# Joins of 64-row blocks laid out by value head, and the loads of layer 1's FFN weights moved into layer 1's order

## The chip, the cores and the metric

The kernel runs on one core of one Trainium2 chip. It is one Bass/Tile program. The metric is device microseconds (us) of one execution, as the median over several runs. A change of about 0.2% of this kernel's time (3.5 us) is about what its measurement can tell from no change.

## What is computed

The input x holds 2 batches of 512 tokens with 256 features (f32). Four layers follow one another, each of the form `x = x + attention(layernorm(x)) + ffn(layernorm(x))`:

- layer 0: attention with 16 query and 4 key heads, and a mixture of 8 experts of which each token takes 2
- layer 1: ALiBi attention, and a gated FFN with Hadamard transforms (weights up, gate and down, together W1F, 3 MB)
- layer 2: linear attention, and a second mixture of experts (weights W2)
- layer 3: a gated delta rule with 16 key heads and 32 value heads, and an FFN whose weights come from a look-up table

The delta rule works in chunks of 64 tokens in the reference. Cut to what matters here:

```python
L = -matmul(k_beta, k.T) * decay            # strictly lower triangular, one per head and chunk
attn = solve_triangular(eye - L, eye, lower=True)
v_intra = matmul(attn, v_beta)
k_cumdecay = matmul(attn, k_beta * exp(g_cum))
# then a scan over the chunks carries a state from chunk to chunk
```

The inverse `attn` of a unit lower triangular matrix is what the changed code computes.

## The kernel before

**The order of the work.** Every part of the kernel is a generator that issues a few instructions and yields. For layers 0 to 2 the order in which the generators advance is written out by hand in strings (ORDER0, ORDER1, ORDER2, L63 on): `weave_in` (L342) takes the next step of the stream that each letter names. In layer 3 every stream has a list of places (JOIN, L1607, is the one of the joins), and `weave_at` (L334) goes through all of them in the order of place. The scheduler is told to keep the order. Each engine, and each queue of DMA requests on SyncE (SP) or GpSimd (POOL), then works strictly in the order in which its instructions were issued. All ordinary matmuls go through the helper `mm` (L116), so they are told apart by the names of their operands.

**Layer 3.** The kernel uses chunks of 128 tokens. A unit is one key head and one batch: 2 value heads x 4 chunks = 8 matrices (NM) of 128x128 to invert. There are 32 units. For the first 24, roughly, the work of several units stands side by side: PE projects and convolves (pxv, pxq, pz), VectorE (DVE) runs the 31-step solve of the 32x32 diagonal blocks (tmp, xx, L1340 to L1343), and the scan of an older unit runs on PE, DVE and ScalarE (ACT).

`join(n)` (L1360 to L1412) puts the inverse of a 128x128 matrix together out of the inverses of its four 32x32 diagonal blocks, for all 8 matrices of a unit, in ten steps:

- ten DMAs on SP fetch the 32x32 inverses and the blocks of the matrix between them: dc, ml (2), U (4), dw (2), m6 (1)
- the 32-joins: twice 16 matmuls of 32x32 into one PSUM bank, p5, with a copy between them (q5); they alternate between row groups 0 and 64 of the array. ACT writes the results into U (L1397)
- a DVE transpose of 32x256 (L1399) puts the off-diagonal blocks of the upper 64x64 inverse into dw
- the 64-joins: 8 matmuls `p6 <- m6, dw`, all of whose operands lie in partitions 0 to 63; an ACT copy of 64x512 to q6 (L1406), which lies in partitions 64 to 127; 8 matmuls `p6 <- q6, U`, all of whose operands lie in partitions 64 to 127; an ACT multiplication by -1 of 64x512 into U (L1411)

m6 and q6 are the two halves of one tile. dw has 64 partitions and room for 8 matrices. An f32 matmul shows as two records in the profile, so a batch of 8 shows as x16.

**The boundary of layers 0 and 1.** In layer 0 each of 23 blocks of gathered rows goes through an expert (L583); its result is written to DRAM as ys (L626, on SP). When the last one has landed, `gathered` (L391) fetches each token's two rows by indirect DMAs on POOL (back, L396) and DVE adds them to x (L401). Then layer 1 begins with its normalisation. Between the two layers' code stands the load of all of layer 1's FFN weights, as one DMA of 3 MB (w1f_sb, L660), and that of W2 (L667), both on SP. `route` (L249) finds each token's experts, places and shares (`found`, L328).

## The time and the profile before

| what | us |
|---|---|
| median of the runs (lowest to highest) | 1743.78 (1742.91 to 1745.04) |
| the profiled execution, its own time | 1752.05 |
| its span, first to last instruction | 1750.3 |
| PE busy between 657 us and the end (layer 3, 1093 us) | 1046.25 |
| DVE busy in the same stretch | 893.01 |
| ACT busy in the same stretch | 740.44 |
| PE busy between 263 and 306 us (the boundary, 43 us) | 30.96 |

Times in views count from the span's start. Layer 0 lies at about 0 to 285 us, layer 1 at 293 to 526, layer 2 at 526 to 657, layer 3 behind that. PE is the matmul unit, PEld its loading of weights, PEclk the clock that was granted to it as a share of full speed; over the whole execution it was 0.977. A group such as `p<-dw,m 64*64 64x64 f32 x16` gives output and operands, the array's rows and columns, the moving operand's shape and the count of records. A chain is the work that ended last, followed back from the end, step by step, to what released it.

### The profile page before, as it was taken

How to read it: one execution, taken by the hardware profiler on the slowest of the kernel's cores; microseconds unless marked ns; L12 is line 12 of the kernel's file. 1: busy time of each engine (PE TensorE's matmuls, PEld its weight loads, DVE VectorE, ACT ScalarE, POOL GpSimd, SP SyncE). 2: the span in 40 equal slices, each digit the busy share in tenths (PEclk: the TensorE clock that was granted, in tenths of full speed). 3: DMA queues.
4: the chain of work that ended last, by engine and by line, in shares of the span. 5: the costliest groups of instructions: out<-in, count | busy, mean ns of one | idle time of the engine just before them, and what ended most of it. 6: DMA issues, size and time to landing. Idle time of an engine off the chain costs nothing.

```text
span 1750.3 us, 31855 instructions
## 1 busy us (share of the span) xinstructions
PE 1671.0 (95%) x11576; PEld 1193.0 (68%) x11576; DVE 1382.7 (79%) x3021; ACT 1003.1 (57%) x2638; POOL 246.0 (14%) x208
## 2 busy tenths in 40 slices
PE   7999997999999997979999999999999999999996
PEld 4377873656665664546777777777777777777775
DVE  6886556977767884778989889899899898886662
ACT  4644232854621113435777777777777778667674
POOL 3400004000000001101111121212121212011111
PEclk8999998999999997989999999999999999999998
DMA  5366743000002002756464555545645545334310
GB/s 199 139 241 240 257 169 142 14 1 1 1 1 94 1 1 69 217 159 181 136 184 135 162 156 152 174 136 146 191 131 162 155 151 158 87 87 111 88 49 24
DMA packets 258204, 214.53 MB, mean 123 GB/s; under 512 B 160769, under 2 KB 222721, under 8 KB 254721
## 3 DMA queue, kind: packets, MB, share of 16 engines
q1 hardware_dynamic: 256512, 208.31, 39.2%
q0 software_dynamic: 1536, 4.20, 0.7%
q8 instruction: 92, 1.51, 0.3%
q14 instruction: 64, 0.52, 0.1%
HBM read 152.69 MB, written 59.77 MB: 121 GB/s over the span
## 4 chain that ended last, share of the span: by engine, by line
PE 75%; DVE 18%; issue 3%; DMA 2%; ACT 2%; SPq 0%; POOL 0%; POOLq 0%; DVEq 0%; ACTq 0%
PE po L116 9%; PE pv L116 8%; PE pc L116 7%; PE pw L116 5%; PE pxv L116 5%; PE pz L116 5%; PE p L116 5%; PE ph L116 4%; PE pl L116 3%; PE pd L116 3%; DVE tmp L1340 3%; PE pxq L116 3%; PE pg L116 2%; PE pu L116 2%; PE pp L116 2%
## 5 line engine op out<-in xcount | busy, mean ns | idle before, releaser
L1259 DVE SCALAR_TENSOR_TENSOR cvv<-pxv,cols,cvv 128x511 f32<-128x511 f32 (+2 forms) x192 | 142.7, 746 | 5.2 <-ACT cvv L1256 0.3
L116 PE MATMUL po<-wo,yT 128*128 128x256 f32 x512 | 127.9, 394 | 2.3 <-ACT yT L1585 2.3
L197 POOL TENSOR_TENSOR rr<-ss,c_sb 128x8 f32<-128x8 f32 x32 | 58.1, 1815 | 497.2 <-DVE ss L1570 497.2
L116 PE MATMUL pxv<-xnT,wg 128*128 128x512 f32 x256 | 122.9, 604 | 0.0
L116 PE MATMUL pz<-wz,xnT 128*128 128x256 f32 x512 | 121.1, 379 | 0.0
L1340 DVE TENSOR_TENSOR tmp<-mb,xx 128x31 f32<-128x31 f32 (+15 forms) x248 | 106.8, 431 | 1.5
L1343 DVE TENSOR_TENSOR xx<-xx,tmp 128x31 f32<-128x31 f32 (+15 forms) x248 | 101.0, 407 | 8.5
L116 PEld LDWEIGHTS po<-wo,yT 128*128 128x128 f32 x512 | 94.4, 194 | 15.0 <-ACT yT L1585 3.2
L372 DVE SCALAR_TENSOR_TENSOR lw<-is,rows,lw 128x536 f32<-128x536 bf16 (+1 forms) x150 | 99.8, 665 | 5.3
L550 ACT ACTIVATE ex<-pl 128x512 f32<-128x512 f32 x128 | 66.6, 602 | 58.0 <-PE pl L116 58.0
L116 PEld LDWEIGHTS pz<-wz,xnT 128*128 128x128 f32 x512 | 92.3, 190 | 9.9
L1445 POOL TENSOR_TENSOR qg<-qk,qg 128x1024 f32<-128x1024 f32 x32 | 75.7, 2364 | 152.7 <-issue 41.8
L116 PE MATMUL pc<-w,aT 128*128 128x128 f32 x512 | 94.7, 277 | 0.0
L1286 ACT ACTIVATE e<-e,lnb 128x128 f32<-128x128 f32 x256 | 80.6, 390 | 15.6 <-POOL e L1280 15.3
L1516 DVE SCALAR_TENSOR_TENSOR r<-pw,negeg,tv 128x128 f32<-128x128 f32 x192 | 58.2, 345 | 36.4 <-PE pw L116 35.2
L1567 ACT ACTIVATE sq<-xf 128x128 f32<-128x128 f32 x256 | 80.1, 313 | 6.7 <-DVE xf L1552 0.7
L1577 ACT ACTIVATE xf<-xf,rr 128x128 f32<-128x128 f32 x256 | 81.4, 391 | 3.9 <-POOL rr L197 3.8
L116 PEld LDWEIGHTS pc<-w,aT 128*128 128x128 f32 x512 | 78.5, 194 | 2.1 <-DVE aT L1447 0.4
L1526 ACT ACTIVATE rb<-pw,bd 128x128 f32<-128x128 f32 x192 | 60.1, 365 | 26.8 <-PE pw L116 24.3
L1259 DVE SCALAR_TENSOR_TENSOR cvk<-pxk,cols,cvk 128x511 f32<-128x511 f32 (+2 forms) x96 | 71.5, 745 | 4.4 <-ACT cvk L1256 2.3
L116 PE MATMUL pc<-st,qg 128*128 128x128 f32 x384 | 74.6, 276 | 0.0
L1259 DVE SCALAR_TENSOR_TENSOR cvq<-pxq,cols,cvq 128x511 f32<-128x511 f32 (+2 forms) x96 | 71.7, 747 | 2.2
(327 smaller groups left out, 4047.9 us busy)
## 6 DMA issues: line engine op xcount, KB each, us to landing
e<-in_E SPq DMA_DIRECT2D x23, 1536.0 KB, 6.6
e<-g_rows SPq DMA_DIRECT2D x32, 512.0 KB, 4.6
m_dram<-mT SPq DMA_DIRECT2D x32, 512.0 KB, 3.5
e_dram<-e SPq DMA_DIRECT2D x32, 512.0 KB, 4.8
e1l<-e_dram SPq DMA_DIRECT2D x32, 512.0 KB, 3.6
qg<-g_rows SPq DMA_DIRECT2D x32, 512.0 KB, 3.7
k_dram<-k SPq DMA_DIRECT2D x32, 256.0 KB, 2.0
qk<-k_dram SPq DMA_DIRECT2D x32, 256.0 KB, 2.6
```

Source lines behind the costliest of these rows:

```text
L116: nc.tensor.matmul(o, lhsT, rhs, start=first, stop=last)
L372: nc.vector.scalar_tensor_tensor(lw[:, at], is_j, lut_j, lw[:, at], ALU.mult, ALU.add)
L550: nc.scalar.activation(exs[k // 2][:, k % 2], pls[k], AF.Exp, scale=HD**-0.5)
L1259: nc.vector.scalar_tensor_tensor(cv[:, back:], px[:, : S - back], conv[:, h, j, 3 - back : 4 - back], cv[:, back:], ALU.mult, ALU.add,)
L1286: nc.scalar.activation(e1f[:, m], e1f[:, m], AF.Exp, bias=lnb[:, h, b, m // C, m % C : m % C + 1])
L1340: nc.vector.tensor_tensor(t, bcast(mb[:q, j, j + 1 :], [q, r, k], 2), bcast(X[:q, j, :k], [q, r, k], 1), op=ALU.mult)
L1343: nc.vector.tensor_tensor(X[:q, j + 1 :, :k], X[:q, j + 1 :, :k], t, op=ALU.subtract)
L1445: nc.gpsimd.tensor_tensor(qg, bcast(qk[:, 0], [P, 2, S], 1), qg, op=ALU.mult)
L1516: nc.vector.scalar_tensor_tensor(r[i], pw[:, 0, i], negeg[:, h, b, i, c : c + 1], tv[i][:, c, :], ALU.mult, ALU.add)
L1526: nc.scalar.mul(wb[:, i], pw[:, 1, i], bd[:, h, b, i, c : c + 1])
L1567: nc.scalar.activation(sq, xfs[c // 2][:, c % 2, i], AF.Square, accum_out=ss[:, c, i : i + 1])
L1577: nc.scalar.mul(xf[:, j, i], xf[:, j, i], rr[:, c + j, i : i + 1])
```

## The change

**The joins.** The 64-joins are laid out by value head. The first head's four chunks have their operands in partitions 0 to 63 and the second head's in 64 to 127. Both batches of matmuls alternate between the two: top rows write the low half of p6, low rows the top half. dw and m6 become tiles of 128 partitions for four chunks, and q6 a tile of its own; a new tile, ub, holds a second copy of the lower 64x64 inverse of the second head, since that head's second join has its operands in partitions 0 to 63. The number of matmuls is the same. The transpose is done in two halves, the copy to q6 becomes 128x256, the last multiplication becomes two of 64x256, a multiplication of 32x128 into ub is added, and the DMAs of a unit go from 10 to 15. The places of JOIN stay as they were.

**The loads.** W1F is requested in two DMAs, the down part (1 MB) first and then up and gate (2 MB), by a stream of its own in layer 1's order, W2 by another one. By the issued instructions, the 1 MB goes out ahead of the last ys write and the 2 MB behind it; before, all 3 MB went ahead of the last.

**The orders.** The strings ORDER0 and ORDER1 are replaced, and `found` is filled in earlier for share and place, later for "of".

```diff
 ORDER0 = (
-    "#####$######u$''*$*$$'$$*$$(''$(*)'$,()*(,%))'(**,,)%%(%%(%))0%%000111..%1%22%-2..2&t--55&55--,&/666"
+    "#####$$######$$'u'$'*$$*$'$($*')*(($/'*)'),(,%(),*%()*,%%)()0%%%%%0001%11.12u..222.55-55t-6&&+666,&-"
...
 ORDER1 = (
-    "(((%%(**&%-*)--)--.+.-.-+%O-/-.+%...-//.'000./)/.'/%/%///)///022/0002&0%0000030223321224&&&442233&33"
+    "**'*+,*'/#+(/-/#'/,,/''00//0-/-1'Q10'//01000002'$+(22111+1)1111114241422(((222222255524444446(6655(("
...
         w1f_sb = w1fp.tile([P, NW1F], F32, name="w1f_sb")
-        nc.sync.dma_start(w1f_sb, a["W1F"])
...
         w2_sb = w2p.tile([P, NW2], F32, name="w2_sb")
-        nc.sync.dma_start(w2_sb, a["W2"])
+
+        def load_w2():
+            nc.sync.dma_start(w2_sb, a["W2"])
+            yield
...
+        def load_ffn():
+            for at in (slice(W1F["down"][0], NW1F), slice(0, W1F["down"][0])):
+                nc.sync.dma_start(w1f_sb[:, at], a["W1F"][:, at])
+                yield
+
...
-        streams = []
+        streams = [load_ffn(), load_w2() if 2 in layers else iter(())]
...
-        dw = l3c.tile([H, NM, H], F32, name="dw")
+        dw = l3c.tile([P, C, H], F32, name="dw")
+        ub = l3c.tile([H, C, H], F32, name="ub")
         us = [l3c.tile([P, NM, P], F32, name=f"U{n}") for n in range(3)]
-        for t in [dw] + us:
+        for t in [dw, ub] + us:
             nc.gpsimd.memset(t, 0.0)
...
-            m6q6 = wk.tile([P, NM, H], F32, tag="m6", bufs=1, name=f"m6{u}")
-            m6, q6 = m6q6[:H], m6q6[H:]
+            m6 = wk.tile([P, C, H], F32, tag="m6", bufs=1, name=f"m6{u}")
+            heads = [(slice(i * H, (i + 1) * H), slice(i * C, (i + 1) * C)) for i in range(2)]
...
+            for at, ms in heads:
+                for lo in (0, SB):
+                    nc.sync.dma_start(
+                        dw[at.start + lo : at.start + lo + SB, :, lo : lo + SB], inv[lo : lo + SB, ms]
+                    )
+                nc.sync.dma_start(m6[at], mv[:H, ms, H:])
             for lo in (0, SB):
-                nc.sync.dma_start(dw[lo : lo + SB, :, lo : lo + SB], inv[lo : lo + SB])
-            nc.sync.dma_start(m6, mv[:H, :, H:])
+                nc.sync.dma_start(ub[lo : lo + SB, :, lo : lo + SB], inv_t[H + lo : H + lo + SB, C:])
...
+            nc.scalar.mul(ub[:SB, :, SB:], p5[H : H + SB, 0, C:], -1.0)
             yield
-            nc.vector.transpose(dw[SB:, :, :SB], U[:SB, :, SB:H])
+            for at, ms in heads:
+                nc.vector.transpose(dw[at.start + SB : at.stop, :, :SB], U[:SB, ms, SB:H])
...
-            p6 = ps(f"p6{u}").rearrange("p (n t) -> p n t", n=NM)
-            for m in range(NM):
-                mm(p6[H:, m, :], m6[:, m, :], dw[:, m, :])
+            p6 = ps(f"p6{u}").rearrange("p (w c t) -> p w c t", w=2, c=C)
+            (top, _), (low, _) = heads
+            for c in range(C):
+                mm(p6[low, 0, c], m6[top, c], dw[top, c])
+                mm(p6[top, 0, c], m6[low, c], dw[low, c])
             yield
-            nc.scalar.copy(q6, p6[H:])
+            q6 = wk.tile([P, C, H], F32, tag="q6", bufs=1, name=f"q6{u}")
+            nc.scalar.copy(q6, p6[:, 0])
             yield
-            for m in range(NM):
-                mm(p6[:H, m, :], q6[:, m, :], U[H:, m, H:])
+            for c in range(C):
+                mm(p6[top, 1, c], q6[low, c], U[low, c, H:])
+                mm(p6[low, 1, c], q6[top, c], ub[:, c])
             yield
-            nc.scalar.mul(U[:H, :, H:], p6[:H], -1.0)
+            for at, ms in heads:
+                nc.scalar.mul(U[:H, ms, H:], p6[at, 1], -1.0)
```

## The prediction, made before the changed kernel was run

> **What bounds the kernel now.** I read the page from the top. Its first part says that TensorE (PE) is busy for nearly the whole span, and its chain of work that ended last says the same.

> ```profile
> PE 1671.0 (95%) x11576; PEld 1193.0 (68%) x11576; DVE 1382.7 (79%) x3021; ACT 1003.1 (57%) x2638; POOL 246.0 (14%) x208
> ...
> PE 75%; DVE 18%; issue 3%; DMA 2%; ACT 2%; SPq 0%; POOL 0%; POOLq 0%; DVEq 0%; ACTq 0%
> ```

> Three quarters of the chain is PE and 18% VectorE (DVE), so work removed from PE should count, except where DVE ends last. The average hides where that is, so I cut four units of layer 3 (119 us of its loop) into quarters. The columns are the busy times of PE, PEld, DVE, ACT and POOL.

> ```profile
> 1010.80:1040.51 29.71, 29.71 (x240) 23.32 (x239) 26.09 (x56) 22.18 (x64) 6.42 (x4) 1.00 0.62 184
> 1040.51:1070.22 29.71, 29.44 (x237) 22.71 (x235) 29.05 (x58) 22.09 (x63) 5.38 (x4) 1.00 0.50 143
> 1070.22:1099.93 29.71, 29.46 (x232) 22.76 (x230) 28.70 (x58) 22.14 (x63) 5.70 (x4) 1.00 0.50 142
> 1099.93:1129.64 29.71, 29.71 (x257) 23.38 (x250) 25.10 (x50) 24.28 (x65) 5.25 (x5) 1.00 0.59 158
> ```

> PE is full everywhere, but in the two middle quarters DVE is within 0.66 and 1.01 us of full as well. There a shorter PE stream gains little. The chain agrees: from about 1034.9 to 1077 it runs through DVE instructions.

> Next I read PE's timeline around one unit's joins. The columns are start, duration of the group, and what it is.

> ```profile
> 1010.13 0.69 PE L116 MATMUL p<-dc,ml 32*32 32x32 f32 x32
> 1010.75 1.99 PE L116 MATMUL po<-wo,yT 128*128 128x256 f32 x8
> ...
> 1022.64 1.14 PE L116 MATMUL p<-dw,m 64*64 64x64 f32 x16
> 1023.71 0.70 PE L116 MATMUL pc<-rb,tk 128*128 128x256 f32 x2
> ...
> 1027.40 1.14 PE L116 MATMUL p<-U,m 64*64 64x64 f32 x16
> 1028.47 0.70 PE L116 MATMUL pw<-st,qk 128*128 128x256 f32 x2
> ```

> From start to next start, 8 matmuls (16 records) of a 64-join take 1.07 us: 67 ns a record. The 16 matmuls (32 records) of a 32-join take 0.62 us: 19.4 ns a record. The 32-joins already alternate between two row groups, 0 and 64; the 64-joins keep one row half throughout.

> **The joins.** The count of matmuls stays at 16 per unit in two batches; only their order over row halves changes. What does alternating give? Full 128x128 matmuls (pc, 2 records in 0.22 us) cost 110 ns for 128 columns, so 32 columns would need about 27 ns and 64 about 55. The 32-join's 19.4 is below its 27, so two row groups do run at once there. A pair of its records takes 39 ns, 12 above 27; a lone 64-join record takes 67, also 12 above 55. So I take the spacing of one row group as its columns plus 12 ns, and two groups as sharing it: 67/2 = 33.5 ns a record, an estimate. The bounds: 19.4 x 64/32 = 39 ns scaled from the 32-join on one side, 33.5 on the other; without any overlap 67, and the full array's 110 as the worst row. I take 36.5, between the two nearest. A batch then takes 0.58 instead of 1.07 us, 0.49 less (0.45 to 0.53).

> How many of the 64 batches count? In the chain, read in stretches of 20 us over layer 3, 49 batches stand as pieces of their own, two of them here (columns: start, us):

> ```profile
> 1022.71 1.07 PE p L116 x16
> ...
> 1027.47 1.07 PE p L116 x16
> ```

> The missing ones fall mostly into the DVE stretches, about one unit in four. Gain: 49 x 0.49 = 24 us (22 to 26; were all 64 to count, 64 x 0.53 = 34).

> The side costs in each unit:
> - ScalarE: the 64x512 copy and mul go (0.581 + 0.576 = 1.16 us). In come a 128x256 copy, two 64x256 muls (0.37 each by the w copy of 128x256, 374 ns, and the 32x256 U mul, 375) and one 32x128 mul, at most 0.31 by the 128x128 sq row. Together 1.42, so +0.26 us. ACT has 5.4 to 7.6 us idle per quarter above, which hides it; unhidden, 32 x 0.26 = 8 us. A change in latency between the joins matters little: the first and second batch are 4.8 us apart on PE.
> - DVE: one 32x256 transpose of 434 ns becomes two of 32x128. Bounds 0 (halves exactly) and 0.43 (no shorter for being narrower); I take +0.15, as fixed parts dominate such short rows. It counts where DVE ends last, some 8 to 16 units: 1 to 2 us. Elsewhere the 3.6 to 4.6 us that DVE has left per quarter cover it.
> - SP's queue: 10 DMAs per unit become 15, at 0.30 to 0.45 us each, so the requests behind them are issued up to 2.2 us later. Behind them stand writes that wait anyway: from 900 to 1480 SP waits 72.8 us for DVE's k in 19 waits (longest 4.7) and 60.4 for aT in 15, about 4 us a time. The joins' own data lands some 8 us before the first 32-join. So I cost it at nothing; without that cover it is up to 2.2 us a unit. One spot (1128.9 to 1129.6) has no slack. The ub DMAs wait for the previous unit's second join, as m6's did, but that is long over when they are issued.
> - POOL: one memset more during layer 2's end, where the four present ones take 0.5 to 0.9 us beside other work: 0.

> When PE gets shorter, DVE becomes the bound for a little longer on either side of its stretches. In the light quarters DVE has slack for 0.5 us per batch several times over, so I take off only 2 us for this. Layer 3: -24 + 1 + 2 = -21 us.

> [...]

> **The boundary of layers 0 and 1.** The chain there (start, us, what):

> ```profile
> 263.32 0.27 ACT y L624
> 263.60 0.02 issue
> 263.61 9.66 DMA ys<-y
> ...
> 277.98 2.70 DMA back<-ys,iplace
> ...
> 281.94 3.25 DVE rden L569
> ...
> 286.03 7.47 PE pp L116 x26
> ```

> The last write of an expert's rows takes 9.66 us to land, although the median of ys<-y is 3.7. SP's queue shows why: the 3 MB load of W1F goes out at 263.14, just ahead of it at 263.61, and shares the DMA engines. PE then stands idle for 9.36 us until 286.03. In the change only 1 MB goes ahead of that write and the other 2 MB follow it. From e_in (1536 KB in 6.6 us) and W1F (3072 KB in 9.7), 1 MB takes about 5.5 us, so the last ys lands near 269.3 instead of 273.3. The gathers behind it now run beside the 2 MB. They were 2.70 us alone and 5.05 in the second row of them; I let a part of the 4 us go, but the second batch's wait (295.13, 5.05 us) moves too. I take -4.5 us. Bounds: 0, if the gathers lose what the write wins, and -8, if PE's whole hole but the normalisation goes. The down and up weights are first needed well inside layer 1's FFN, so a later 2 MB harms nobody; W2 keeps its place after them, and layer 2 is 200 us away.

> The new order strings of layers 0 and 1 move ops between engines' queues. From 88 to 263 us PE is 174.91 of 175 busy, and from 306 to 526 it is 218.79 of 220, so there a reordering can neither win nor, if it keeps PE fed, lose much. Between 0 and 88 PE has 13 us idle, held by the same loads and exponentials; route's results share and place only become known earlier. I take 0, bounds -2 and +2.

> **The sum.** -21 - 4.5 + 0 = -25.5 us. Against the profiled execution (1752.05 us, with a span of 1750.3) that is 1726.5. That execution lies 8.3 us above the median of the runs shown, 1743.78, and the same difference from it gives **1718 us**.

> **The rivals.**
> - *DVE swallows half.* Only the two light quarters of each four units gain: 32 batches x 0.49 = 16, less 2 to 4 us of DVE's extra, less the boundary's 4.5: about -17, 1727; with a boundary of 0, 1731. For it: 29.05 of 29.71. Against it: three units in four have their batches on the chain. Chance 0.2.
> - *More than I take.* 33.5 ns, nearly all batches, and 6 to 8 us at the boundary: -31 to -40, 1704 to 1713. For it: in the four units PE is never less than 99% busy. Chance 0.1.
> - *The halves don't overlap.* At 67 ns the joins gain nothing and DVE and ACT lose 2 us; the boundary's 4.5 leave -2.5: 1741, within what a measurement calls no change (0.2%, 3.5 us). [...] Against it: the 32-joins. Chance 0.08.
> - *The halves hinder each other.* [...] At 110 ns, a full-array pass, 49 x 16 x 43 ns = 34 us, +2 - 4.5: about 1775. It ends slower from about 75 ns a record on, since 784 records x 7.7 ns make the 6 us that lie between -2.5 and +3.5. Only the 32-joins speak against it. Chance 0.07, in which I count the SP queue's 2.2 us a unit as well.

> My forecast, 1711 to 1725, has the other 0.55. The range from 1705 to 1733 holds it, the first rival and most of the second. Faster by over 0.2%: 0.55 + 0.2 + 0.1 = 0.85; within 0.2%: 0.08; slower: 0.07.

> **What would show it.** The two 64-join groups on PE's timeline should go from 1.07 to 0.54 to 0.62 us with the same 16 records. At 1.07 the overlap step is wrong. PE busy in layer 3 falls by some 30 us while its share stays at about 95%; if the four-unit period of 119.0 us shrinks by less than 2 us with DVE above 29 in more than two quarters, the first rival is right. At the boundary the last ys should land in about 6 us, and PE's first pp start near 281.5. If the waits of SP for k and aT vanish and PE waits for qk or e, the queue was not free. A period of 115.5 us with 64-joins of 0.58 would confirm the whole.

## The result, and the profile after

The changed kernel takes 1745.15 us (median of 12 runs, 1739.23 to 1749.54), the kernel before 1743.80 (12 runs, 1739.37 to 1745.47). The ratio is 1.0003 with a 95% interval of 0.999 to 1.0016: no difference that can be measured. The prediction was 1718, with a range from 1705 to 1733.

The profiled execution of the changed kernel took 1745.70 us (span 1743.9). The one of before, 1752.05, lay above all of the 12 runs of before, so I compare stretches that several profiles share rather than whole spans. Busy time and the engines' part of the chain, from the page of the changed kernel:

```profile
PE 1648.9 (95%) x11576; PEld 1166.9 (67%) x11576; DVE 1378.0 (79%) x3053; ACT 1002.8 (58%) x2702; POOL 245.2 (14%) x209
...
PE 75%; DVE 13%; DMA 4%; ACT 4%; issue 3%; SPq 2%; POOL 1%; POOLq 0%; DVEq 0%; ACTq 0%
```

PE lost 22 us of work with the same number of instructions; behind 657 us, in layer 3, it lost 26 (1046.25 to 1020.30; the forecast was some 30). But the chain now holds 4% of DMA, 4% of ACT and 2% of SP's queue, where it held 2%, 2% and 0%. Something that is not PE has come in. PE's timeline of the changed kernel shows it around the joins (start, duration, group, and in brackets idle time and what ended it):

```profile
1014.13 1.98 PE L116 MATMUL pxv<-xnT,wg 128*128 128x512 f32 x4 [0.94 <-DMA wg<-in_qkvz]
...
1020.24 1.16 PE L116 MATMUL pkk<-k 128*128 128x128 f32 x8 [1.97 <-DVE k L247]
...
1023.50 0.68 PE L116 MATMUL p<-dw,m 64*64 64x64 f32 x16
1024.11 0.70 PE L116 MATMUL pc<-rb,tk 128*128 128x256 f32 x2
```

The 64-join itself is as forecast: 0.61 us to the next start instead of 1.07. The second batch has two names for its operands, so there the timeline shows the two halves side by side (three records):

```profile
1027.96 0.22 PE L116 MATMUL p<-U,q 64*64 64x64 f32 x1
1027.97 0.22 PE L116 MATMUL p<-ub,q 64*64 64x64 f32 x1
1028.02 0.22 PE L116 MATMUL p<-U,q 64*64 64x64 f32 x1
```

A pair starts every 0.06 us, and within a pair the halves start 0.01 us apart. In front of the first batch PE stands still for 0.94 us, until wg has landed, and for 1.97 us, until DVE has made k. Before, neither wait was there. Cut into units (from one first 32-join to the next; columns as in the prediction), the changed kernel looks like this:

```profile
1007.55:1039.71 32.16, 29.25 (x237) 22.21 (x236) 25.53 (x57) 22.07 (x67) 5.27 (x3) 1.00 0.60 177
1039.71:1069.70 29.99, 29.50 (x237) 22.13 (x236) 29.32 (x59) 22.28 (x67) 5.47 (x4) 1.00 0.44 123
1069.70:1098.73 29.03, 28.82 (x237) 22.07 (x236) 28.33 (x59) 22.40 (x67) 5.69 (x5) 1.00 0.57 166
1098.73:1127.24 28.51, 28.51 (x237) 22.24 (x236) 24.94 (x50) 23.98 (x68) 6.22 (x5) 1.00 0.57 156
```

Before, the same four units took 29.43, 30.01, 29.97 and 29.43 us. The last two have won 0.9 each, and one unit in four, the one whose join comes right behind a solve, has lost 2.7; further on that unit takes 33.34, 31.32 and 33.08 us. In it no engine is full: PE 29.25 and DVE 25.53 of 32.16. The chain of work that ended last leads from PE's joins through SP's queue (start, duration, what):

```profile
1007.62 0.65 PE p L116 x32
1008.27 0.26 SPq L1396
...
1009.04 0.58 SPq L931
...
1009.66 0.61 SPq L938
...
1010.32 0.61 SPq L939
...
1010.98 5.44 DMA e<-g_rows
...
1016.53 1.10 POOL e L1292
...
1017.97 0.97 ACT e L1298 x3
1018.94 0.52 ACT thk L1278
```

L1396 is the two requests for ub, two of the five new ones, L931 is wk, L938 and L939 are wg. Only behind them goes out the broadcast e, 5.44 us to landing, then POOL masks it, ACT takes its exponential, and only behind that, in ACT's order, stands thk, from which DVE makes k, for which PE waits. In that unit the solve's two stores, its four loads of mb (4.6 us) and the join's requests fill SP's queue without a gap. Its five requests for the second head (dw twice, m6, ub twice):

```profile
1005.34 1.92 SPq L1391 DMA_DIRECT2D dw<-xn_dram  x2
1007.30 0.58 SPq L1394 DMA_DIRECT2D m<-m_dram  x1
1007.98 1.02 SPq L1396 DMA_DIRECT2D ub<-xt_dram  x2
```

These five take 3.7 us of the queue. The same chain of before, from the timelines of SP, POOL, ACT and DVE:

```profile
1010.83 0.60 SPq L1214 DMA_DIRECT2D e<-g_rows  x1
...
1015.67 1.09 POOL L1280 TENSOR_SCALAR_AFFINE_SELECT e<-e 128x1024 f32<-128x1024 f32 x1 [6.08 <-DMA e<-g_rows]
...
1017.98 0.61 ACT L1266 ACTIVATE thk<-cvk 128x512 f32<-128x512 f32 x1
...
1018.63 0.69 DVE L247 SCALAR_TENSOR_TENSOR k<-thk,cvk 128x512 f32<-128x512 f32 x1 [1.48 <-ACT thk L1266]
```

PE's pkk started at 1019.48 there. Each link waited for the one before it: k was done at 1019.32, so the slack was 0.2 us. Measured from the unit's first 32-join (1010.13 before, 1007.55 after), e goes out at +0.70 before and at +3.43 after.

SP's own waits do not give this away. Between 900 and 1480 us it waits 72.8 us for k in 19 waits before, and 89.8 in 20 waits after: a later e makes k later, and SP waits for k all the longer.

### The profile page after: what moved, and what is told of

It is laid out like the page before. It is cut to its first block, busy times and chain, and to the rows that moved or that the text cites. A ratio compares the mean times of both kernels' runs of the same rounds, so it can differ in the third digit from the quotient of the medians.

```text
span 1743.9 us, 32156 instructions
## 1 busy us (share of the span) xinstructions
PE 1648.9 (95%) x11576; PEld 1166.9 (67%) x11576; DVE 1378.0 (79%) x3053; ACT 1002.8 (58%) x2702; POOL 245.2 (14%) x209
## 3 DMA queue, kind: packets, MB, share of 16 engines
q0 software_dynamic: 1536, 4.20, 0.7%
## 4 chain that ended last, share of the span: by engine, by line
PE 75%; DVE 13%; DMA 4%; ACT 4%; issue 3%; SPq 2%; POOL 1%; POOLq 0%; DVEq 0%; ACTq 0%
PE po L116 8%; PE pv L116 8%; PE pc L116 6%; PE pw L116 6%; PE pz L116 5%; PE pxv L116 4%; PE ph L116 4%; PE pl L116 3%; PE p L116 3%; PE pxq L116 3%; PE pd L116 3%; PE pg L116 2%; PE pxk L116 2%; PE pu L116 2%; PE pp L116 2%
## 5 line engine op out<-in xcount | busy, mean ns | idle before, releaser
L116 PE MATMUL pxv<-xnT,wg 128*128 128x512 f32 x256 | 126.3, 618 | 6.5 <-DMA wg<-in_qkvz 6.5
L116 PE MATMUL po<-wo,yT 128*128 128x256 f32 x512 | 126.6, 391 | 2.3 <-ACT yT L1609 2.3
L116 PE MATMUL pz<-wz,xnT 128*128 128x256 f32 x512 | 121.1, 380 | 0.0
L116 PEld LDWEIGHTS po<-wo,yT 128*128 128x128 f32 x512 | 93.8, 193 | 14.6 <-ACT yT L1609 3.1
L1355 DVE TENSOR_TENSOR xx<-xx,tmp 128x31 f32<-128x31 f32 (+15 forms) x248 | 92.7, 374 | 8.5
L116 PEld LDWEIGHTS pz<-wz,xnT 128*128 128x128 f32 x512 | 92.5, 191 | 9.8
L116 PE MATMUL pc<-w,aT 128*128 128x128 f32 x512 | 95.1, 278 | 0.6 <-DVE aT L1471 0.6
L116 PEld LDWEIGHTS pc<-w,aT 128*128 128x128 f32 x512 | 78.7, 195 | 2.7 <-DVE aT L1471 1.0
L116 PEld LDWEIGHTS pxv<-xnT,wg 128*128 128x128 f32 x256 | 48.3, 199 | 43.1 <-issue 33.3
L116 PE MATMUL pc<-st,qg 128*128 128x128 f32 x384 | 74.7, 277 | 0.0
```

The costliest lines, as they stand in the source:

```text
L116: nc.tensor.matmul(o, lhsT, rhs, start=first, stop=last)
L1355: nc.vector.tensor_tensor(X[:q, j + 1 :, :k], X[:q, j + 1 :, :k], t, op=ALU.subtract)
```

## The experiments

Theory Q: the five added requests of a join delay wg and e in SP's queue in each fourth unit, and this takes back what the new joins give. Rival V: PE's saving is swallowed by DVE and ACT, which got more to do. All kernels were timed beside the kernel before.

**Requests later.** The requests for dw, m6 and ub, which are needed last, go behind those of wk, wg and e:

```diff
+            yield
             for at, ms in heads:
                 for lo in (0, SB):
...
-        JOIN = [7.869, 8.266, ...
+        JOIN = [7.869, 8.090, 8.266, ...
```

> The changed kernel, but the eight requests for dw, m6 and ub go out in a step of their own at place 8.090, behind the loads of wk and wg and the broadcast of e. Theory Q (SP's queue: in each fourth unit, where the solve's stores and loads precede the join, the five added requests delay wg and e, and POOL, ACT, DVE's k and then PE wait): that unit falls from 33.1 us to between 28.5 and 29.5, the other three stay at 28.5 to 29.0; seven such units give 25 to 30 us, so 1716 to 1721. Theory V (DVE and ACT are the bound, by their added instructions): the unit stays at 32 to 33 us and the time within 1742 to 1748.

Measured: 1724.93 us, ratio 0.9881 (0.9867 to 0.9896); the gain on the changed kernel is 20 us. Four units of this kernel:

```profile
999.96:1028.47 28.51, 28.51 (x238) 22.22 (x237) 26.46 (x57) 22.19 (x67) 5.41 (x4) 1.00 0.69 199
1028.47:1058.34 29.87, 29.50 (x238) 22.11 (x237) 29.20 (x59) 22.31 (x67) 5.35 (x3) 1.00 0.48 137
1058.34:1088.14 29.80, 29.02 (x238) 22.06 (x237) 29.11 (x59) 22.41 (x67) 5.84 (x5) 1.00 0.55 149
1088.14:1116.65 28.51, 28.51 (x237) 22.22 (x237) 24.62 (x50) 24.08 (x68) 5.98 (x5) 1.00 0.58 159
```

The unit behind the solve takes 28.51 us, with PE never idle, so theory Q holds; the gain of 20 us is under its 25 to 30. The two middle units are why: there DVE has 29.2 of 29.87 us, and they win only 0.15 us on before. That is theory V's mechanism, for half of the units of the loop. From the start of the first unit's first 32-join to that of the last unit's, the changed kernel takes 904.5 us and this one 884.7 (before: 902.4): all of the 20 us lie within the units.

**Only the added requests.** The joins of before, with dw and m6 fetched in twice as many parts and two loads into a tile that nothing reads:

```diff
-            for lo in (0, SB):
-                nc.sync.dma_start(dw[lo : lo + SB, :, lo : lo + SB], inv[lo : lo + SB])
-            nc.sync.dma_start(m6, mv[:H, :, H:])
+            for ms in (slice(0, C), slice(C, NM)):
+                for lo in (0, SB):
+                    nc.sync.dma_start(dw[lo : lo + SB, ms, lo : lo + SB], inv[lo : lo + SB, ms])
+                nc.sync.dma_start(m6[:, ms], mv[:H, ms, H:])
+            for lo in (0, SB):
+                nc.sync.dma_start(ub[lo : lo + SB, :, lo : lo + SB], inv_t[H + lo : H + lo + SB, C:])
```

> The kernel before, its joins unchanged, with only the five added requests in each unit: dw and m6 fetched in twice as many parts, and two loads into a tile that nothing reads. Theory Q: the unit behind the solve goes from 29.4 to 32 to 33.5 us, the others stay at 29.4 to 30.0; seven of them add 18 to 28 us, so 1762 to 1772. Theory V: no change, 1741 to 1747.

Measured: 1763.07 us, ratio 1.0101 (1.0082 to 1.012). Units behind a solve take 32.41, 32.55, 32.34, 32.07 and 32.59 us, the others 29.4 to 30.3. The chain of this kernel is the same one (the L1383 is the second request for ub):

```profile
1008.60 0.43 SPq L1383
...
1011.00 5.11 DMA e<-g_rows
...
1016.23 1.10 POOL e L1281
...
1019.19 0.70 DVE k L247
...
1019.93 1.16 PE pkk L116 x8
```

So five requests that do no work cost 19 us, about the amount that the new joins win once the requests stand later.

**The two halves of the change alone.** The new joins with the old orders and loads, and the other way round:

> The new joins with the old orders and loads of layers 0 and 1. The profiles put the boundary's gain at 4.6 us and 1.3 more ahead of it, so 1749 to 1752 if that holds outside of the profile; 1744 to 1747 if the boundary is worth nothing. Theories Q and V both say 33 us for each fourth unit here.

> The new orders and loads of layers 0 and 1 with the old joins. The last write of ys should land in about 5 us instead of 9.7 and the first matmul of layer 1 start 6 us earlier: 1737 to 1740 if the two profiles stand for the other executions, 1742 to 1746 if the profile of before was only unlucky there. Layer 3 keeps its 119.0 us for four units by both theories.

Measured: 1745.17 us, ratio 1.0009 (0.9997 to 1.0022), for the joins alone, and 1744.97, ratio 1.0 (0.9989 to 1.0011), for the boundary alone. Each is worth nothing, within 2 us. The boundary's loads and its orders were not tried apart.

**Without the alternation.** Each batch runs the four matmuls of one row half and then the four of the other, once in the changed kernel and once with the later requests:

```diff
             for c in range(C):
                 mm(p6[low, 0, c], m6[top, c], dw[top, c])
+            for c in range(C):
                 mm(p6[top, 0, c], m6[low, c], dw[low, c])
...
```

> The changed kernel with its requests where they are, but each batch of 64-joins first runs the four matmuls of the one row half, then the four of the other. The group should take 1.07 us again. Theory Q: the time is that of the kernel before with five added requests, 1760 to 1766; the alternation's 18 to 20 us were there in the changed kernel and only covered the queue's loss. Theory V (PE's saving swallowed by other engines): 1743 to 1748, nothing to lose.

> The kernel with late requests (1724.9), but without the alternation. By theory Q queue and alternation add up, so 18 to 21 us above it, 1743 to 1746, with no unit above 30.1 us. If the late requests had freed more than the queue's loss, it would lie under 1740.

Measured: 1756.06 us, ratio 1.0055 (1.0039 to 1.0071), and 1737.34, ratio 0.995 (0.9933 to 0.9967). Both lie under what was expected, by 4 and 6 us. The reason is in the first one's timeline of PE, at a first and at a second batch:

```profile
1054.82 0.96 PE L116 MATMUL p<-dw,m 64*64 64x64 f32 x16
1055.71 0.48 PE L116 MATMUL pc<-rb,tk 128*128 128x256 f32 x1
```

```profile
1059.39 0.50 PE L116 MATMUL p<-U,q 64*64 64x64 f32 x5
1059.68 0.27 PE L116 MATMUL p<-ub,q 64*64 64x64 f32 x1
1059.73 0.22 PE L116 MATMUL p<-U,q 64*64 64x64 f32 x1
```

The batch takes 0.89 us, not 1.07: the second half (ub) starts when the first (U) has issued five of its eight records, so the two overlap by themselves. The alternation as such is worth 0.28 us a batch, and that made 11 us (1756.06 against 1745.15) and 12 us (1737.34 against 1724.93); by the ratios to the kernel before, which was timed beside each of them, 9 and 12. The rest of the joins' 20 us is what the layout by head wins without it: 0.18 us a batch, and 8 us between the next kernel's ratio, 0.9996, and 0.995. The alternation adds up with the queue in both places.

**Requests later, but the old joins.** The missing corner:

```diff
+            yield
             for lo in (0, SB):
                 nc.sync.dma_start(dw[lo : lo + SB, :, lo : lo + SB], inv[lo : lo + SB])
...
-        JOIN = [7.869, 8.266, ...
+        JOIN = [7.869, 8.090, 8.266, ...
```

> The kernel before, its joins and their ten requests unchanged, but the three requests for dw and m6 go out at place 8.090, as in the kernel with late requests. Theory Q: the kernel before lost nothing to the queue (its unit behind the solve takes 29.4 us like others), so no gain: 1741 to 1747, and the 20 us of the kernel with late requests are the alternation's. If e was late in the kernel before as well, it is 1730 to 1740.

Measured: 1742.94 us, ratio 0.9996 (0.9981 to 1.0011). The later requests alone win nothing; the 20 us are the new joins'.

**Another queue.** The five requests for the second head go out on ScalarE (`nc.scalar.dma_start`):

> The changed kernel, but the five requests for the second head (dw twice, m6, ub twice) are issued by ScalarE instead of SP, at the same place. SP then has ten per unit as before. Theory Q: the unit behind the solve falls to 28.5 to 30.5 us, 1722 to 1732, unless ScalarE's own order is held up by them: it has 5 to 7 us free in a unit and five issues take some 2 us. Theory V: 1742 us or more, for ACT has more to do than in the changed kernel.

Measured: 1787.69 us, ratio 1.0228 (1.021 to 1.0247): a miss. ACT's and PE's timelines of this kernel:

```profile
1006.00 1.19 ACTq L1392 DMA_DIRECT2D dw<-xn_dram  x2
1007.23 0.58 ACTq L1395 DMA_DIRECT2D m<-m_dram  x1
1008.20 0.80 ACTq L1397 DMA_DIRECT2D ub<-xt_dram  x2
1009.05 0.60 ACT L1506 ACTIVATE zz<-pz 128x512 f32<-128x512 f32 x1 [3.34 <-DMA mb<-m_dram]
```

```profile
1011.06 0.70 PE L116 MATMUL pc<-rb,tk 128*128 128x256 f32 x2 [1.75 <-ACT w L1553]
```

ACT computes nothing for 3.34 us, of which the five issues are 2.6, at a place where its results are waited for: PE waits 1.75 us for w. Each unit, not one in four, takes 30.4 to 33.9 us between 860 and 1520 us. The expectation had set these issues (2 us) against ACT's idle time in a unit, and not against the place in its order. Here SP, which had no computing to do, was the better place, once the order in it was right.

**One PSUM bank or two.** The kernel with later requests, p6 in two banks, one for each row half:

> The kernel with late requests (1724.9), with p6 in two PSUM banks, one for the results of each row half; the copy to q6 becomes two of 64x256 (+0.37 us of ScalarE in a unit). If the one bank costs nothing, the groups stay at 0.61 us and the time at 1723 to 1727. If the halves disturbed each other in one bank, the groups fall toward 0.54 us, and 64 x 0.07 gives some 3 to 4.5 us: 1720 to 1722.

Measured: 1726.25 us, ratio 0.9894 (0.9871 to 0.9918). The pairs of records start 0.05 to 0.06 us apart with two banks as with one. So the halves, which write different partitions of p6's one bank, overlap in it as they do in two, and two banks gain nothing here (1726.25 against 1724.93 us).

**The boundary.** Its chain in the changed kernel:

```profile
261.83 4.86 DMA ys<-y
...
279.66 8.86 PE pp L116 x26
```

The last write lands after 4.86 us instead of 9.66, and PE is idle for 4.78 us ahead of pp instead of 9.36. So the 4.5 us of the prediction are there, at that place. But pp takes 8.4 to 8.9 us where it took 7.5 before, and the granted clock is the reason I tried: five matmuls of 128x512, whose result nothing reads, go into PE's hole in the kernel with later requests (and ten into the hole of 9.6 us with the old boundary):

```diff
                 for g in range(4):
+                    if (b, c, j, g) == (WB, WC, 0, 3):
+                        warm = psf_tile("warm")
+                        for _ in range(5):
+                            mm(warm, sel, encs[b, 0])
                     mm(pp[:, j], encs[b, g][:, blk(c + j)], wog[:, g], g == 0, g == 3)
```

> The kernel with late requests, and five matmuls of 128x512 whose result nothing reads, in PE's hole of 4.9 us ahead of layer 0's last projection. Theory: the boundary's gain goes to the lower granted clock behind the hole; with PE kept busy the 26 records of pp fall from 8.4 to 5.7 to 6.5 us, the clock stays above 0.9 from 276 to 308 us, and layer 2 begins 2 to 4 us earlier: 1721 to 1723. Rival: layer 1 is longer through its new order, and the time stays at 1724 to 1726.

> The kernel with late requests (1724.9), but with the old orders of layers 0 and 1 and the old loads of W1F and W2. If the boundary's 4.6 us of earlier start are lost again within layer 1, as the run with only the boundary says, it stays at 1723 to 1727. If the boundary is worth its 4.5 us once layer 3 is freed, 1728 to 1731.

> The same, with ten matmuls of 128x512 whose result nothing reads in PE's hole of 9.6 us ahead of layer 0's last projection. If the lower granted clock is what eats the boundary's gain, the 26 records of pp fall from 7.45 to about 5.9 us here too, 1.5 to 2.5 us in all, so 1722 to 1724, and the new boundary with PE kept busy (1720.8) stays 2 to 4 us below it. If the new order of layer 1 itself is the longer one, this kernel is as fast as that one or faster, 1721 or less.

| with later requests | median, us | ratio (interval) |
|---|---|---|
| new boundary | 1724.93 | 0.9881 (0.9867 to 0.9896) |
| old boundary | 1726.40 | 0.989 (0.9871 to 0.9908) |
| new boundary, hole filled | 1720.81 | 0.9856 (0.9838 to 0.9874) |
| old boundary, hole filled | 1723.14 | 0.9872 (0.9853 to 0.9891) |

PE around the hole with the new boundary, without the added matmuls and with them, and last with the old boundary and ten of them:

```profile
279.63 8.41 PE L116 MATMUL pp<-wog,enc 128*128 128x256 f32 x26 [4.85 <-DVE enc L572]
```

```profile
274.14 4.46 PE L116 MATMUL warm<-enc,sel 128*128 128x512 f32 x10
278.98 5.88 PE L116 MATMUL pp<-wog,enc 128*128 128x256 f32 x26 [0.38 <-DVE enc L572]
```

```profile
274.55 8.75 PE L116 MATMUL warm<-enc,sel 128*128 128x512 f32 x20
284.41 5.88 PE L116 MATMUL pp<-wog,enc 128*128 128x256 f32 x26 [1.11 <-DVE enc L570]
```

Filled, pp takes 5.88 us and the clock stays at 1.00 through it; unfilled, the granted clock is 0.50 from within the hole to behind it, with either boundary: from 278.0 to 284.8 us in the first kernel of the table, with PE busy for 5.2 us of it, and from 278.7 to 288.9 in the second, with PE busy for 3.8. The changed kernel has 0.50 from 280 to 285 us as well, and the kernel before from 280 to 289. So the shorter hole has the shorter low clock, but more work under it. Filling is worth some 3 to 4 us by the medians, though the intervals of the ratios overlap. The forecast of a clock above 0.9 up to 308 us did not come true: from 297.95 to 301.35 us it is 0.50 once more. Ahead of this second stretch of 0.50 stands no idle time as long as the holes (4.85 and 9.57 us), only a wait of 1.49 us.

The new boundary stays 1.5 to 2.3 us ahead by the medians, within their intervals. With the hole filled, layer 1's first transposition (pxn) starts 5.4 us earlier than with the old boundary (284.7 against 290.1), but the one of layer 2's second batch only 2.1 (519.0 against 521.1). So 3.3 us go inside layer 1, most of them here (new boundary, then old, both filled):

```profile
297.49 0.66 PE L771 MATMUL pt<-c_sb,lo 128*128 128x128 f32 x2 [1.49 <-ACT lo L762]
297.94 3.59 PE L116 MATMUL pw<-w_sb,xnT 128*128 128x256 f32 x8
```

```profile
300.72 0.62 PE L767 MATMUL pt<-c_sb,lo 128*128 128x128 f32 x2 [0.15 <-ACT lo L758]
301.71 1.99 PE L116 MATMUL pw<-w_sb,xnT 128*128 128x256 f32 x8 [0.38 <-DVE qq L703]
```

In the new order PE waits 1.49 us for ACT's lo, 0.15 in the old one, and behind that wait stands the second stretch of 0.50, which makes pw 1.6 us longer. The wait alone does not explain that stretch: the changed kernel has it too, 1.58 us long, and its clock stays at 1.00 from 296 to 304 us. What brings the clock down there is open.

The kernel with later requests and the hole filled, 1720.81 us, beats both kernels: 1.4% below before.

## Why the prediction was wrong

- **The step that failed** is the one on SP's queue: "Behind them stand writes that wait anyway [...] I cost it at nothing". SP's waits for k were taken as slack. They were none: right behind the join's requests stand no writes but the loads of wk and wg and the broadcast e, and k is made from e's landing by way of POOL and ACT. Whoever delays e delays k, and SP then waits for k even longer (89.8 us instead of 72.8). So the sign "If the waits of SP for k and aT vanish" looked at the wrong place. The average of 4 us over all units hid the one unit in four whose queue is full. The issues were also longer than the "0.30 to 0.45 us each": the five took 3.7 us in the unit shown, not 2.2. The price was 2 to 4 us in each of these units; the requests alone cost 19 us, and moving eight of the requests gave 20 back.
- The prediction saw one spot without slack, 1128.9 to 1129.6, and gave "up to 2.2 us a unit" as the price without the cover, but put it into a rival of 7% and not into the range. That spot is the request for e in the next unit behind a solve, whose first 32-join starts at 1128.97: the same spot comes back in every fourth unit. Had one unit in four been charged with the queue's time, 8 x 2.2 = 18 us, the forecast would have been 1736; PE lost more, 0.94 + 1.97 us in the unit shown, as wg and e were both late.
- **The overlap** was right: 38 ns a record (0.61 us for 16) against the forecast 36.5, in one bank. The picture behind it, 12 ns beside the columns of every record, was not: in both kernels the records of one half start 58 ns apart (107 between the first two), the two halves run side by side at that pace, and some 0.14 us of 1.07 and of 0.61 is spent once per batch.
- **The joins' worth** was nearly right once the queue was free: 20 us of 21. But the split was another, so that the sum agrees is in part luck: the last eight units won about 0.9 each but for one (0.45), the two light units of four also, and the two that DVE fills 0.15, where I had left out about one unit in four. The prediction's own quarters showed DVE near full in two of four, and its stretch on DVE, 1034.9 to 1077, is 42 of 119 us; the count of 49 batches did not follow them.
- **The side costs** were right: two transposes of 0.303 us instead of one of 0.434, +0.17 (forecast +0.15); on ACT 0.351 + 2 x 0.373 + 0.269 us against 0.581 + 0.582, +0.20 (forecast +0.26).
- **The boundary** was right at its place, 4.8 us less for ys and 4.6 us less idle time on PE, and wrong at its end: 0 within 2 us, where the sum had 4.5. "If it keeps PE fed" was the condition that I set for the new order of layer 1, and it does not quite keep PE fed there; a shorter hole, too, still brings the clock down, with more work under it. The sum had no term for the clock.
- The rival that DVE swallows half was half right, for a gain that the queue had taken already; the two rivals that the halves don't overlap or hinder each other were refuted by the timeline.

## What to carry to other kernels

On SP's full queue the added requests cost their issue time for everything behind them (3.7 us for five; e went out 2.7 us later). And the queue's later waits were no slack, since k, which it waits for, is itself made from e, which comes through that queue (72.8 us of waits for k before, 89.8 after). So follow the first operand behind the added requests to the engine that waits for it. Look at slack in the unit where the queue is fullest, not at its mean. Put small loads that are needed late behind the loads that the next unit needs first (here eight requests, worth 20 us with the new joins; three with the old joins were worth nothing).
